# Attention of a conv/SSM, attention and experts kernel in a written order: three batches in flight, sums moved between engines, ranks batch by batch

## The chip, the cores and the metric

The kernel runs on one core of one Trainium2 chip. The metric is device microseconds for one launch. Three runs of the kernel before gave 3556.59 us as their median (3550.72 to 3560.29). Engines are named as in the profile: PE (matrix products and transposes; PEld is its weight load), DVE (vector), ACT (scalar), POOL (GpSimd), SP (which only issues transfers here). Each engine works through its own queue in order and waits on the others by semaphores.

## The reference, cut to what matters

Input is `x` of 4 batches, each 32x32 positions of 256 channels, so 1024 tokens a batch. Layer 0 is a convolution with a state-space scan; it makes up most of the time and is not changed. Layer 1 is attention without a softmax over tokens, then 16 experts of which each token takes two:

```python
# t: (4, 1024, 256); _ln_t: layer norm over the channels
q, k, v = split(_ln_t(t) @ W_qkv + b_qkv)
q = q - mean(q);  k = k - mean(k)                       # over channels
q2, k2 = q*q, k*k
k2 = l2norm(k2 / (sum(k2) + 1e-7), over tokens)
q2 = l2norm(q2 / (sum(q2) + 1e-7), over channels)
kv = einsum('bnc,bnd->bcd', k2, v)
t = t + (v + einsum('bnc,bcd->bnd', q2, kv) / sqrt(N)) @ W_out + b_out
u = _ln_t(t)
probs = softmax(u @ gate_w + gate_b)                    # 16 experts
w, idx = top_k(probs, 2);  w = w / sum(w)
t = t + sum over the two: w * (silu(u @ w1[e]) * (u @ w2[e])) @ w3[e]
```

So per token the kernel needs the sum of squares of q and k, the sum of fourth powers of q, and per channel two sums over all tokens of a batch: of k2 and of k2 squared.

## The kernel before, in words

Tokens lie on the 128 partitions, in groups of 128: a batch is NT = 8 groups, all four together NTA = 32. `t_all` (128 x 32 x 256, fp32) holds the residual stream in SBUF. Everything is fp32.

**The scan** (up to about 2767 us) is ordered by hand. Its last unit leaves four groups (TPB = 4) of the last batch unfinished: `last_half` (L1137) gives them their output product later, inside attention.

**Attention** (L1109 to L1346) is one loop over the batches, L1158. Its order is not written by hand: the framework places the instructions of neighbouring batches on the queues, within what buffers allow. Steps for a batch, with their lines:

- layer norm statistics of the 8 groups on DVE (`statistics`, L1125: `bn_stats` and `bn_aggr`, then a square root on ACT and a reciprocal on DVE); ACT scales the groups to `xh` (L1165); PE transposes them four to a PSUM bank (`transposed`, L114) and DVE copies them out (`xhT`, L1169);
- for each group the q/k product (`pqk`, L1179), the bias on DVE (L1184), both squares in one ACT instruction of 512 elements (`sq`, L1187), both sums by one reduction on DVE (`sums`, L1188), the fourth power with ACT's own accumulator (L1190), the output bias on POOL (L1193), the product of x with W_v W_out (`pv`, L1196) and its addition on DVE (L1200). W_v and W_out are multiplied beforehand, so v is never formed;
- k2 scaled on ACT (L1209) and squared there (`ksq`, L1212); q's norm (L1215 to L1219); q2 transposed, copied out by DVE (`q2T`, L1223);
- the product of k2 with x over tokens (`pkv`, L1231), copied out (L1236); the sums over tokens folded on DVE from 8 groups to 1, for `ksq` and for `k2` (L1241 to L1245), then summed over partitions by PE with a vector of ones (`pkn`, L1251), root and copy (L1254, L1255); the product with W_v W_out, scaled (`kvw`, L1262 to L1269);
- for each group the product of q2 with `kvw` (`po1`, L1276) and its addition, scaled by q's norm (L1280); statistics again; the expert input `xe` on DVE (L1288), stored to DRAM by one transfer of 1 MB (L1292); `xe` transposed, copied out by ACT (L1296); the gate's product (`pgT`, L1303), turned back (`pg`, L1310);
- the gating on DVE with one exponential on ACT (L1311 to L1344): top two of 16 experts as one-hot rows in `hots`, and their weights.

`last_half` is called ahead of the second batch.

**The router** (L1358 to L1463) starts when all batches are gated. It counts the pairs (token, expert) of all 32 groups at once: a 128 x 512 one-hot sum (L1362), two products for totals and for ranks within a group (L1367, L1369), a scan along the groups (L1372), the number of 128-row blocks of each expert and where each expert starts (L1381 to L1386), the expert of each of NBLK = 79 blocks (`eid`, L1389 to L1394), and each pair's slot (L1396 to L1418). Then, in four chunks of 16 groups, it forms one-hot rows of the place in the block (`qh`, L1429) and of the block (`ih`, L1433), and sums group and partition numbers by PE into a list by slot (`pgp`, L1444). `src` and `dst` (L1451 to L1463) are the rows to gather and to scatter.

**The experts** (L1468 to L1568, an order written by hand) go through 74 blocks (more only if needed): SP reads the block's expert from `eid` and loads w1, w2, w3, 512 KB each, four blocks ahead into pools of six buffers (`wp`, opened at L1468, after the router's pools are closed), POOL gathers the block's rows by an indirect transfer (L1488), PE multiplies, POOL scatters the result to `yd` (L1539). **The final sum** (L1572) adds two weighted rows to each token and stores the output.

The order around the change is set by the engines' queues, by the number of buffers of each tile, and by PSUM's banks: `pt` 2, `pq` 3, `po` 2 and `pk` 1.

Of the kernel before, what the change touches and what calls it, by code (L numbers as in the profile page):

```python
# [8 lines left out]
F32 = mybir.dt.float32  # L9
# [24 lines left out]
def conv_ssm_attn_moe_kernel(ctx: ExitStack, tc: tile.TileContext, a: dict, out: bass.AP):  # L34
# [1027 lines left out]
    hots = [l1.tile([P, NTA, NE], F32, name=f"hots{k}") for k in range(2)]  # L1062
# [8 lines left out]
    def counted(n, lo, step, name):  # L1071

        t = l1.tile([P, n], F32, name=name)
        nc.gpsimd.iota(
            t, [[step, n]], base=lo, channel_multiplier=0,
            allow_small_or_imprecise_dtypes=True,
        )
        return t

    nbe = L * NB // BS  # L1080
    bounds = counted(nbe, 0, BS, "bounds")
    blocks = counted(NBLK, 0, 1, "blocks")

    places = l1.tile([P, BS], BF16, name="places")
    nc.vector.tensor_copy(places, counted(BS, 0, 1, "places_f"))
    blocks_h = l1.tile([P, NBLK], BF16, name="blocks_h")
    nc.vector.tensor_copy(blocks_h, blocks)

    groups = l1.tile([P, NTA], BF16, name="groups")
    nc.vector.tensor_copy(groups, counted(NTA, 0, 1, "groups_f"))  # L1090
    part_pk = l1.tile([P, 2], F32, name="part_pk")
    nc.gpsimd.iota(
        part_pk, [[1, 2]], base=1, channel_multiplier=2,
        allow_small_or_imprecise_dtypes=True,
    )
    spare = l1.tile([P, 1], F32, name="spare")
    nc.gpsimd.iota(
        spare, [[1, 1]], base=2 * NB * L + 1, channel_multiplier=1,
        allow_small_or_imprecise_dtypes=True,
    )  # L1100
    before = l1.tile([P, P], F32, name="before_t")
    make_upper_triangular(nc, before, 1.0, diag=False)
    every = l1.tile([P, P], F32, name="every_t")
    nc.vector.memset(every, 1.0)
    keep = l1.tile([P, NE, NTA], F32, name="keep")
    nc.vector.memset(keep, 1.0)
    nc.vector.memset(keep[:, :, 0:1], 0.0)

    with tc.tile_pool(name="wa", bufs=1) as wa, tc.tile_pool(name="att", bufs=1) as att, \  # L1109
            tc.tile_pool(name="sm", bufs=2) as sm, \  # L1110
            tc.tile_pool(name="ps_b", bufs=2, space=PSUM) as ps_b:
        tbs = [t_all[:, b * NT : (b + 1) * NT, :] for b in range(NB)]
        for b in range(NB - 1):
            nc.sync.dma_start(out=tbs[b], in_=rows(td, b))
        nc.sync.dma_start(out=tbs[-1][:, :TPB, :], in_=rows(td, NB - 1)[:, :TPB, :])
        nc.sync.dma_start(out=tbs[-1][:, TPB:, :], in_=rows(xf, NB - 1)[:, TPB:, :])
        wg = load_rows("L1_ffn_gate_w", CK, NE, wa)
        gb = load_bcast("L1_ffn_gate_b", NE, wa)
        iota = wa.tile([P, NE], F32, name="iota")
        nc.gpsimd.iota(  # L1120
            iota, [[1, NE]], base=NE, channel_multiplier=0, allow_small_or_imprecise_dtypes=True
        )
        wqk, wvo, bqk, bvo, bout = made["mats"]

        def statistics(tb, tag, n=NT):  # L1125

            mv = sm.tile([P, n, 2], F32, name="ln_mv", tag=tag + "mv")
            for i in range(n):
                st = sm.tile([P, 6], F32, name="ln_st", tag=tag + "st")
                nc.vector.bn_stats(st, tb[:, i, :])  # L1130
                nc.vector.bn_aggr(mv[:, i, :], st)
            rs = sm.tile([P, n], F32, name="ln_rs", tag=tag + "rs")
            nc.scalar.activation(rs, mv[:, :, 1], AF.Sqrt, bias=eps5)
            nc.vector.reciprocal(rs, rs)
            return mv, rs

        def last_half():  # L1137

            ysb = made["ysb", len(units) - 1]
            _, rs = statistics(ysb, "ln1", TPB)  # L1140
            for j in range(TPB):
                t = tbs[-1][:, TPB + j, :]
                nc.gpsimd.tensor_tensor(t, t, b_o, ALU.add)
                ps = ps_b.tile([P, BANK], F32, name="ps_l", tag="po")
                for m in range(DK):
                    nc.tensor.transpose(ps[:, blk(m, P)], ysb[:, j, blk(m, P)], ident)
                yT = sm.tile([P, BANK], F32, name="yT")
                nc.vector.tensor_copy(yT, ps)
                po = ps_b.tile([P, C], F32, name="po_l", tag="po")
                for m in range(DK):  # L1150
                    nc.tensor.matmul(
                        po, yT[:, blk(m, P)], w_o[:, m, :], start=(m == 0), stop=(m == DK - 1)
                    )
                nc.vector.scalar_tensor_tensor(
                    t, po, rs[:, j : j + 1], t, ALU.mult, ALU.add
                )

        for b in range(NB):  # L1158
            if b == 1:
                last_half()  # L1160
            tb = tbs[b]
            _, rs = statistics(tb, "ln2")
            xh = att.tile([P, NT, C], F32, name="xh", bufs=2)
            for i in range(NT):
                nc.scalar.activation(xh[:, i, :], tb[:, i, :], AF.Copy, scale=rs[:, i : i + 1])  # L1165
            xhT = att.tile([P, CK, L], F32, name="xhT", bufs=2)
            transposed(
                ps_b, xh, NT,
                lambda ck, half, ps: nc.vector.tensor_copy(xhT[:, ck, blk(half)], ps), "pt",  # L1169
            )  # L1170


            sq = att.tile([P, NT, 2, C], F32, name="sq", bufs=2)
            sums = sm.tile([P, NT, 2], F32, name="sums")
            q4 = sm.tile([P, NT], F32, name="q4")
            for i in range(NT):
                pqk = ps_b.tile([P, 2, C], F32, name="pqk", tag="pq", bufs=3)
                for ck in range(CK):
                    nc.tensor.matmul(  # L1179
# [439 lines left out]
```

## Time and profile before

| what | value |
|---|---|
| median of three runs | 3556.59 us (3550.72 to 3560.29) |
| the profiled execution | 3564.42 us, span 3562.6 us, granted PE clock 0.973 |
| scan, to about | 2767 us |
| first q/k product of the four batches | 2779.5, 2841.9, 2912.8 and 2975.0 us |
| first gating step of the last batch | 3034.2 us |
| `src` ready | 3079.4 us |
| first expert product | 3087.7 us |
| last scatter issued | 3520.2 us |
| busy over the whole span | PE 92%, DVE 82%, ACT 78%, POOL 70% |

How to read it: the shares in the last row are means over stages with different limits and hardly speak of attention, which is some 7.5% of the span. The windows are what to read: for a stretch of time, the span, and for each engine its busy time and number of instructions, then PE's granted clock, the share of the transfer engines' time, and GB/s. A group of instructions has its line, engine, operation and shapes, the count, busy time and mean duration, and the idle time of its engine just before. The waits name who waited for whom. Matrix products are pipelined, so their own durations overlap: what one costs in a row of its kind is the time from start to start. DVE's neighbouring instructions overlap by a little in the same way.

### The profile page before, as it was taken

How to read it: one execution, taken by the hardware profiler on the slowest of the kernel's cores; microseconds unless marked ns; L12 is line 12 of the kernel's file. 1: busy time of each engine (PE TensorE's matmuls, PEld its weight loads, DVE VectorE, ACT ScalarE, POOL GpSimd, SP SyncE). 2: the span in 40 equal slices, each digit the busy share in tenths (PEclk: the TensorE clock that was granted, in tenths of full speed). 3: DMA queues.
4: the chain of work that ended last, by engine and by line, in shares of the span. 5: the costliest groups of instructions: out<-in, count | busy, mean ns of one | idle time of the engine just before them, and what ended most of it. 6: DMA issues, size and time to landing. Idle time of an engine off the chain costs nothing.

```text
span 3562.6 us, 62683 instructions
## 1 busy us (share of the span) xinstructions
PE 3292.8 (92%) x23188; PEld 2744.0 (77%) x23188; DVE 2933.6 (82%) x3342; ACT 2764.9 (78%) x4577; POOL 2481.9 (70%) x901
## 2 busy tenths in 40 slices
PE   8999999999999999999999999899999788599995
PEld 4577777887888788878877887788888555498984
DVE  4799999999999999999999999999999776522224
ACT  1799999999999899999999999999999343121110
POOL 0379878987898799879978987998888200133331
PEclk9999999999999999999999999999999899699997
DMA  3332222223332222233332223222222100499996
GB/s 99 108 59 72 61 66 69 70 71 64 76 77 63 73 72 73 67 68 76 71 72 69 67 69 74 61 63 63 67 68 59 59 12 18 157 362 317 301 317 225
DMA packets 423575, 352.38 MB, mean 99 GB/s; under 512 B 194385, under 2 KB 309841, under 8 KB 423266
## 3 DMA queue, kind: packets, MB, share of 16 engines
q1 hardware_dynamic: 403794, 324.56, 31.8%
q0 software_dynamic: 7104, 19.41, 1.6%
q10 hardware_dynamic: 12368, 4.37, 0.5%
q8 instruction: 185, 3.03, 0.3%
q14 instruction: 124, 1.02, 0.1%
HBM read 318.24 MB, written 29.47 MB: 98 GB/s over the span
## 4 chain that ended last, share of the span: by engine, by line
ACT 42%; PE 37%; DVE 9%; DMA 6%; issue 2%; POOL 0%; DVEq 0%; POOLq 0%; ACTq 0%; SPq 0%
ACT da L870 20%; ACT bx L862 18%; PE y L914 8%; PE ps L882 8%; DVE h L893 4%; PE p L1519 4%; DMA yd<-yb,dst 4%; PE ps L877 3%; PE bg L404 2%; DMA xb<-xd,src 2%; PE pf L1531 2%; PE pqk L1179 2%; PE pv L1196 1%; PE ps L404 1%; PE ps_t L120 1%
## 5 line engine op out<-in xcount | busy, mean ns | idle before, releaser
L900 POOL TENSOR_TENSOR h<-h,cb_n 128x2048 f32<-128x2048 f32 x512 | 2143.3, 4193 | 396.6 <-DVE h L893 319.8
L870 ACT ACTIVATE da<-dt,l_conv_a_log_sb 128x512 f32<-128x512 f32 x2048 | 1452.0, 718 | 41.8 <-DVE h L893 40.6
L862 ACT ACTIVATE bx<-dtxT,bT 128x512 f32<-128x512 f32 x1824 | 1308.0, 717 | 17.7 <-DVE dtxT L566 17.7
L893 DVE TENSOR_TENSOR_SCAN h<-da,last,ps 128x512 f32<-128x512 f32 x1024 | 1220.0, 1262 | 27.3 <-PE ps L882 13.6
L914 PE MATMUL y<-ident,h 128*128 128x128 f32 x8192 | 1237.9, 274 | 3.0 <-POOL h L900 3.0
L882 PE MATMUL ps<-ident,bx 128*128 128x128 f32 x7296 | 1171.6, 278 | 74.2 <-DVE h L893 51.7
L893 DVE TENSOR_TENSOR_SCAN h<-da,ps 128x512 f32<-128x512 f32 x1024 | 1170.7, 1201 | 43.1 <-ACT da L870 19.4
L882 PEld LDWEIGHTS ps<-ident,bx 128*128 128x128 f32 x7296 | 854.2, 142 | 299.9 <-DVE h L893 144.9
L914 PEld LDWEIGHTS y<-ident,h 128*128 128x128 f32 x8192 | 968.0, 142 | 3.5 <-POOL h L900 3.5
L877 PE MATMUL ps<-dgb,dtxT 128*128 128x128 f32 x1792 | 387.5, 298 | 31.1 <-DVE h L893 21.9
L877 PEld LDWEIGHTS ps<-dgb,dtxT 128*128 128x128 f32 x1792 | 281.3, 190 | 168.4 <-DVE h L893 88.6
L1525 DVE TENSOR_TENSOR hT<-s,p 128x256 f32<-128x256 f32 x148 | 62.4, 422 | 343.1 <-ACT s L1524 343.1
L1519 PE MATMUL p<-xT,w 128*128 128x128 f32 x2368 | 292.9, 278 | 0.5 <-ACT xT L1508 0.5
L1519 PEld LDWEIGHTS p<-xT,w 128*128 128x128 f32 x2368 | 286.1, 194 | 4.7 <-ACT xT L1508 0.9
L1524 ACT ACTIVATE s<-p 128x256 f32<-128x256 f32 x148 | 56.7, 383 | 277.0 <-PE p L1519 277.0
L1539 POOL DMA_INDIRECT yd<-yb,dst x74 | 73.0, 987 | 271.9 <-DMA yd<-yb,dst 154.5
L404 PE MATMUL bg<-pad,dgc 128*128 128x512 f32 x432 | 221.7, 595 | 2.0 <-ACT yT L642 1.9
L1488 POOL DMA_INDIRECT xb<-xd,src x74 | 72.0, 973 | 133.7 <-DVE dst L1460 109.7
L1531 PE MATMUL pf<-w,hT 128*128 128x256 f32 x592 | 153.5, 382 | 0.1
L1193 POOL TENSOR_TENSOR t_all<-t_all,brow 128x256 f32<-128x256 f32 x32 | 23.2, 747 | 179.7 <-ACT xh L1165 179.7
L1531 PEld LDWEIGHTS pf<-w,hT 128*128 128x128 f32 x592 | 102.2, 193 | 8.2 <-DVE hT L1525 0.5
L1508 ACT COPY xT<-px 128x256 f32<-128x256 f32 x74 | 27.5, 372 | 83.1 <-PE px L1506 83.1
(296 smaller groups left out, 2196.2 us busy)
## 6 DMA issues: line engine op xcount, KB each, us to landing
cb_n<-cd SPq DMA_DIRECT2D x512, 256.0 KB, 3.3
w<-in_L_ffn_w_dram SPq DMA_DIRECT2D x222, 512.0 KB, 6.4
dgc<-diags SPq DMA_DIRECT2D x84, 192.0 KB, 3.1
dgb<-diag_b SPq DMA_DIRECT2D x224, 64.0 KB, 3.1
y<-yd SPq DMA_DIRECT2D x8, 1024.0 KB, 10.2
last<-h SPq DMA_DIRECT2D x256, 2.0 KB, 2.9
diag_b<-zero SPq DMA_DIRECT2D x2, 2048.0 KB, 9.6
xd<-xe SPq DMA_DIRECT2D x4, 1024.0 KB, 4.4
```

What stands on the lines that cost most here:

```text
L404: nc.tensor.matmul(made["bg"].rearrange("p (h w) -> p h w", w=WW), made["dgc", m * 3 + i][:, j, :], pads[m][:, half * ROWS + i : (half + 1 ...
L862: nc.scalar.activation(t, made["dtxT", u][:, j, :], AF.Copy, scale=made["bT", u][:, j, n : n + 1])
L870: nc.scalar.activation(t, made["dt", u][:, m, :], AF.Exp, scale=A[:, m, n : n + 1])
L877: nc.tensor.matmul(t[:, blk(j, P)], made["dtxT", steps[s][0]][:, j, blk(m, P)], made["dgb", s], start=True, stop=True,)
L882: nc.tensor.transpose(t[:, blk(j, P)], made["bx", s, j][:, blk(m, P)], ident)
L893: nc.vector.tensor_tensor_scan(h[:, m, 1:], made.pop(("da", s, m)), made.pop(("dbx", s, m)), 0.0 if seg == 0 else last[b][:, n, m : m + 1] ...
L900: nc.gpsimd.tensor_tensor(h[:, :, :BANK], h[:, :, 1:], over_middle(made["c", s], DK), ALU.mult)
L914: nc.tensor.matmul(made["y", u][j][:, blk(m, P)], made["h", s][:, m, blk(j, P)], ident, is_transpose=True, start=n == 0 and m == 0, stop=n ...
L1488: nc.gpsimd.indirect_dma_start(t, None, xd[:, :], bass.IndirectOffsetOnAxis(src[:, i : i + 1], 0))
L1519: nc.tensor.matmul(p12[:, j, s, :], on[w, i][:, ck, blk(h + j, P)], on["xT", i][:, ck, :], start=(ck == 0), stop=(ck == CK - 1),)
L1531: nc.tensor.matmul(on["pf", i], on["hT", i][:, hk, :], on["w3", i][:, hk, :], start=(hk == 0), stop=(hk == HK - 1),)
L1539: nc.gpsimd.indirect_dma_start(yd[:, :], bass.IndirectOffsetOnAxis(dst[:, i : i + 1], 0), yb, None)
```

## The change

Attention is put under `manual_schedule`, so queues take the instructions in the order of the program, and its steps become small functions that a written loop calls. Iteration `o` finishes batch o (its kv product, `out`), does the q/k part of batch o+1, the gate, routing and ranks of batch o-1, and the statistics and scaling of batch o+2. The last four groups of the scan are turned and multiplied ahead of the first batch's transposes. Batch 0 is loaded in two halves and takes its q/k part by itself, ahead of the loop. The core of the loop, where `n`, `z` and `s` are o+1, o-1 and o+2 if they exist:

```diff
+            turn_next(0); v_out(o, 0); turn_q(o, 0); v_out(o, 1); turn_q(o, 1)
+            first_part(0)                       # q/k of group 0 of batch n
+            turn_e(z, 0); norm_q(o); root(batch[z], "ln3", HT, NT); expert_in(z, 1)
+            turn_next(1); first_part(1); on_with(steps, 2); look_ahead(0, 4)
+            v_out(o, 2); gates(z, 0); turn_e(z, 1)
+            kv(o, 0); on_with(steps, 40); look_ahead(4, 8); gates(z, 1); first_part(2)
+            turn_g(z); steps = route(z)
+            kv(o, 1); on_with(steps, 2); kv_out(o); scale_ahead()
+            v_out(o, 3); on_with(steps, 2); norm_k(o); first_part(3); on_with(steps, 2)
+            kv_w(o); v_out(o, 4); on_with(steps, 1); first_part(4); on_with(steps, 1)
+            k2(n, 0)
+            out(o, 0); on_with(steps, 1); out(o, 1); v_out(o, 5); first_part(5)
+            out(o, 2); on_with(steps, 1); out(o, 3); root(batch[o], "ln3", 0, HT)
+            v_out(o, 6); on_with(steps, 1); first_part(6); expert_in(o, 0)
+            out(o, 4); on_with(steps, 1); first_part(7); v_out(o, 7); fourth(n, 7); k2(n, 1)
+            out(o, 5); on_with(steps, 1); out(o, 6); on_with(steps, 1); out(o, 7)
```

(Joined here to fewer lines; in iteration 0 the missing `z` steps give way to `last_sum` and the constants, and after the last iteration the remaining gate and route steps follow alone.) `on_with(steps, n)` lets the routing of a batch, now a generator of 18 pieces, go on by n pieces.

Work that changes its engine or its form:

```diff
-                nc.scalar.activation(sq[:, i, :, :], qk, AF.Square)
-                nc.vector.tensor_reduce(sums[:, i, :], sq[:, i, :, :], AX.X, ALU.add)
+            for k in range(2):
+                nc.scalar.activation(on["sq"][:, i, k, :], t[:, k, :], AF.Square,
+                    accum_out=on["sums"][:, i, k : k + 1])
...
-                nc.scalar.activation(ksq[:, i, :], k2[:, i, :], AF.Square)
+            nc.gpsimd.tensor_tensor(on["ksq"][:, lo:hi, :], on["k2"][:, lo:hi, :],
+                on["k2"][:, lo:hi, :], ALU.mult)          # four groups at once
...
-                nc.vector.tensor_tensor(four, m[:, : NT // 2, :], m[:, NT // 2 :, :], ALU.add)
-                nc.vector.tensor_tensor(four[:, :2, :], four[:, :2, :], four[:, 2:, :], ALU.add)
-                nc.vector.tensor_tensor(fold[:, k, :], four[:, 0, :], four[:, 1, :], ALU.add)
+                # first half:  two = m[0:2] + m[2:4]                          on GpSimd
+                # second half: two += m[4:6]; two += m[6:8]; fold = two[0] + two[1]
...
-                nc.vector.tensor_scalar(xe[:, i, :], tb[:, i, :], mv[:, i, 0:1], rs[:, i : i + 1],
-                    ALU.subtract, ALU.mult)
+                nc.scalar.activation(on["xe"][:, i, :], tbs[b][:, i, :], AF.Identity,
+                    bias=nm[:, i - lo : i - lo + 1], scale=rs[:, i : i + 1])
```

The expert input is stored by two transfers of 512 KB a batch. The buffers of `sq`, `xe` and `xeT` are their own and single.

Ranks: `route(b)` goes on, after the one-hot rows of its batch, with the sum of both (128 x 128), two products of 128 x 128, a scan over the batch's 8 groups for each expert, the counts of the batches before added (`counts[b]`), each pair's slot within its expert, split into block and place, and the one-hot rows of the places (`qh`, two instructions of 128 x 1024 a batch, kept in SBUF for all batches). What is left for the router after the last batch:

```diff
+        nc.vector.tensor_scalar(nbi, counts[-1], float(BS - 1), None, ALU.add)
+        nc.vector.tensor_single_scalar(nbi, nbi, BS.bit_length() - 1, ALU.arith_shift_right)
...
+        nc.vector.tensor_tensor(
+            pick, hot_all.rearrange("p k g e -> p (k g) e"), over_middle(first, 2 * NTA), ALU.mult
+        )
...
+        nc.vector.tensor_tensor(bh, bf, within, ALU.add)
+        nc.vector.tensor_scalar(done, end, block_p, None, ALU.is_le)
...
+        nc.tensor.transpose(pe, ef, ident)
+        nc.vector.tensor_scalar(eid, pe[:, :NBLK], float(NE - 1), None, ALU.min)
...
-                qh = rt2.tile([P, GC, BS], BF16, name="qh", bufs=2)
-                nc.vector.tensor_tensor(
-                    qh, over_middle(places, GC), over_last(qb[:, k, gs], BS), ALU.is_equal
-                )
```

The four chunks with `ih`, `both` and the products stay. The expert of each block now lies along partitions and is turned by PE into one row. The weights' pool `wp` is opened ahead of the router's pools, so that it shares no memory with them. The constants (number rows, triangular matrix, ones) move from the start of attention into iteration 0.

## The prediction

> **What bounds the kernel now.** I read the windows by stage first (span, then busy PE, PEld, DVE, ACT and POOL, clock, DMA), since the change touches one stretch only: attention with the router (2767.8 to 3080 us), between scan and experts. Whole batches, then the two parts of the router's end:
>
> ```profile
> 2858.00:2915.00 57.00, 48.99 (x191) 31.02 (x191) 35.66 (x84) 23.03 (x56) 5.80 (x8) 0.91 0.06 19
> 2915.00:2977.00 62.00, 53.73 (x209) 34.17 (x208) 42.10 (x107) 25.19 (x61) 5.87 (x8) 0.94 0.05 17
> ...
> 3041.00:3056.00 15.00, 3.37 (x4) 1.18 (x4) 12.43 (x24) 0.00 (x0) 0.00 (x0) 0.61 0.01 2
> 3056.00:3078.00 22.00, 9.14 (x64) 7.90 (x64) 19.67 (x12) 5.41 (x4) 0.00 (x0) 0.50 0.00 0
> ```
>
> A batch takes 62 us; no engine is full, PE (54 with its latencies) is nearest. The router's end is DVE's: 32 busy of 37. The second view cuts one batch into its steps:
>
> ```profile
> 2913.00:2934.00 21.00, 21.00 (x70) 12.49 (x69) 17.94 (x46) 8.35 (x23) 0.00 (x0) 1.00 0.00 1
> 2934.00:2938.00 4.00, 2.42 (x18) 1.70 (x17) 3.84 (x11) 3.29 (x7) 0.00 (x0) 1.00 0.00 0
> 2938.00:2952.50 14.50, 12.10 (x48) 9.29 (x49) 6.63 (x13) 5.37 (x17) 0.00 (x0) 0.88 0.00 0
> 2952.50:2961.60 9.10, 7.72 (x34) 5.47 (x32) 7.80 (x26) 0.00 (x0) 0.00 (x0) 1.00 0.01 2
> 2961.60:2975.00 13.40, 10.49 (x45) 5.09 (x46) 5.83 (x13) 8.18 (x16) 5.87 (x8) 0.87 0.23 78
> ```
>
> Only the first step, q, k and v, fills PE: one token tile each 2.58 us in the timeline, 1.72 for q/k and 0.86 for v. The other 41 us are a chain from engine to engine. The waits (total, times, longest) name its links:
>
> ```profile
> ACT ln_rs L1133 <- DVE ln_mv L1131: 47.2, 5, 12.4
> ACT nk L1254 <- PE pkn L1251: 23.8, 5, 5.9
> DVE xhT L1169 <- PE ps_t L120: 23.4, 4, 7.7
> DVE four L1241 <- ACT ksq L1212: 20.3, 4, 5.1
> ```
>
> So DVE stands until squares of k are done and until the next batch is transposed, and the next batch starts only when this one is gated. Work of another batch could fill these holes.
>
> **The written order: what PE needs.** Per batch, by start-to-start times at full clock: q/k and v 8x2.58 = 20.6; k'x products 32 records x0.215 = 6.9; out products the same 6.9; weighting 1.7; 48 transposes x0.11 = 5.3; gate 8x0.43 = 3.4; its turns, column sums and the new rank products together 2.2. Sum 47. DVE per batch after, by starts (128x512 about 0.62, 128x256 0.35): statistics of input 3.8, evacuations of x and q 5.0, q/k bias 5.0, v 2.8, out with statistics 8x0.86 = 6.9, kv and small ones 3.5, gating 5.5, ranks 5.9 (below): 38. ACT: three squares with accumulators a tile, 24x0.54 = 13 (the fourth-power group shows 0.415 + 0.186, overlapped), two scalings 6.5, expert input 3.4, evacuations 3.2, two table loads 2.6, rest 1.6: 30. POOL from its two rows (128x256 0.75 us, 128x2048 4.19: 1.92 ns an element): squares 2x2.22, six adds of 512 x1.24, folds 2x0.75, bias 8x0.75: 19. So PE becomes the bound, with 47.
>
> What goes from DVE: the sums of squares (32x0.68 = 22 us), the folds (8x2.34 = 19), the expert input (15.6). None shortened PE by itself; they give DVE the room for the new order.
>
> **What it will not reach.** PE waits in its written place for everything made just before: transposes into two banks (0.3 to 0.5 a wait in the timeline), column sums (1.5 now), weights before `out` (0.5 to 1.5), rank products behind DVE. I count 13 such hand-offs of 0.5 in a full iteration, 6.5 us, and 1.5 for GpSimd (below): 8. First and last iteration have less: 5 and 4.6.
>
> GpSimd's new work runs beside DVE. The timeline shows what that can do: eight identical instructions with POOL at work and with POOL idle.
>
> ```profile
> 2962.31 4.31 DVE L1288 TENSOR_SCALAR xe<-t_all,ln_mv,ln_rs 128x256 f32<-128x256 f32 x8
> 2962.52 2.98 POOL L1193 TENSOR_TENSOR t_all<-t_all,brow 128x256 f32<-128x256 f32 x4 [54.73 <-ACT xh L1165]
> ...
> 3023.14 2.68 DVE L1288 TENSOR_SCALAR xe<-t_all,ln_mv,ln_rs 128x256 f32<-128x256 f32 x8
> ```
>
> 1.63 us lost beside 2.98 of POOL, 0.55 each; times 19 us of POOL, at most 10.5 a batch. At the other end, the scan beside a POOL that never rests costs 1.20 to 1.26 (one operand in PSUM), as its groups show: 0. DVE has 9 us of room against PE (47 - 38), so I take 1.5, near the low end: few of the instructions left are of the xe kind, since expert input goes to ACT. The Trainium skill, "SBUF — State Buffer", Who interferes with whom, speaks against the change: an instruction with two SBUF inputs, or in a two-port mode, is blocked for a whole GpSimd instruction, one with an input in PSUM is not. By it only ranks, gating and the one-hot of places collide, some 20 a batch; at half a 1.24 us add each that would be 12 us, DVE at 50 would pass PE's 47, and a full iteration would be near 58.
>
> **The sum for attention** (landing of batch 0, 2767.8, to the last gate's first DVE step, 3034.2: 266.4 now):
> - Head, now 11.7 to the first q/k product. The last half's turns and products come first, in order: chain of copies 0.6, products 1.7, table load 1.28, two scalings 1.7, in all 14.2, and 2.5 for a cold PE (clock 0.50 to 0.71 in these windows): 16.7. In return `last_half` leaves the window 2842 to 2858.
> - q/k of batch 0 alone: PE 13.8, ACT 18.4 (13 + 1.6 + 3.8): 17, ACT's rest passes into the loop.
> - Four iterations: PE 40.9 (no batch behind), 47, 47, 32.4 (none ahead) = 167.3; with waits 5 + 8 + 8 + 4.6: 192.9.
> - From the last `out` to the gate: 11.7 now; half the expert input and transposes are done before, 8.
>
> Sum 234.6: gain 31.8. If no PE wait remained it were 25.6 more.
>
> **Ranks batch by batch.** From the last one-hot (3040.25) to `src` (3079.4) now 39.2 us. What forms the second half, from the DVE groups:
>
> ```profile
> L1429 DVE TENSOR_TENSOR qh<-places,qb 128x2048 bf16<-128x2048 bf16 x4 | 9.1, 2285 | 0.0
> L1437 DVE TENSOR_TENSOR both<-ih,groups 128x1264 bf16<-128x1264 bf16 x4 | 5.9, 1474 | 0.0
> L1433 DVE TENSOR_TENSOR ih<-blocks_h,bh 128x1264 bf16<-128x1264 bf16 x4 | 5.8, 1470 | 0.0
> ```
>
> After, for the last batch alone: sum 0.3, products 0.9, scan on 128 elements 0.36 (not shown; between a 128x128 step at 0.28 and the 512 scan at 1.22, nearer the first), 1.0 for three steps, picks 1.2, slots 0.8, places 2x1.17 = 2.3; then ends 0.9 and 0.2, pick and reduction over 1024 elements 2.4, `bh` and the transposed `eid` 1.0: 11.4 against 15.4. Then four chunks of 2.78 (starts) = 11.1 in place of 20, then 2.3 + 1.9 as now. 26.7: gain 12.5. The first three batches' 5.9 us each lie on DVE under PE. The weights' pool now lies outside the router's, so weight loads follow `eid`, not the end of the router; the first rows' gather took 6.2 us among them. I take 2 us less (between 0 and 3); weights themselves were not late (the first product waited 0.46, for ACT's copy of its rows).
>
> **Small moves.** Batch 0 is loaded by two DMAs, expert input is stored by eight of 512 KB in place of four of 1 MB (4.4 us to landing); SP has nothing else queued until the weights, and the last store lands some 25 us before the first gather: nothing. The constants (nine instructions on POOL, 0.13 to 0.29 each, six on DVE, 1.4 in all) go into iteration 0, where both have room; before, they lay under the end of the scan. POOL's last fold ends an iteration ahead of the first gather in its queue: nothing.
>
> Experts and the final sum keep their instructions; PE is busy 92.5 of 93 in the first expert window, so nothing follows there.
>
> **Sum.** 31.8 + 12.5 + 2 = 46.3. The profiled execution took 3564.42 (span 3562.6), 7.8 above the median of 3556.59; 3518 in its terms, 3510 against the median.
>
> **Rivals.**
> - *PE hardly waits.* For: in the q/k/v step PE shows no hole at all. Waits 4 instead of 25.6, and q/k alone 14: 24.6 more, 3486.
> - *DVE, blocked by GpSimd, sets the pace.* For: the xe rows. DVE 38 + 10.5 and its own in-order waits bring a full iteration back to 62, 7 more, twice, and 6 and 5 in the others: 25 lost, 3535.
> - *Slower: PE's order costs a wait per group.* An order by hand can't step over a late input; the timeline shows today's doing so (gating of one batch among the next one's q/k steps). Some 180 groups of matmuls stand in the four iterations; my waits are 0.14 a group. At 0.40 a group, 72 us, the gain is gone; at 0.5 (the q2T hand-offs of now, everywhere) 90, and 3575. Against: most groups have another batch's input, ready long before.
> - *The change does not do what it says*: the experts absorb the start because loads, not rows, decide. Then 2 to 5 us less; inside the range.
>
> **Chances.** Forecast 0.50, PE without waits 0.22, blocked DVE 0.18, slower 0.07; 0.03 lies near zero. Within 0.3% (10.7 us), about what a measurement of this kernel can tell from no change: 0.03; faster 0.90, slower 0.07. The range reaches from a little under the first rival to a little over the second: 3482 to 3538.
>
> **What would show it.** Right: PE's windows of full iterations near 55 us with 47 of work, clock near 1.0; router end some 27 us with no `qh`; ACT near 60% busy. Wrong: `out` or rank steps on DVE lasting beside POOL; PE waiting on `k2` or `fold`; the first q/k product after 2790. The likeliest error is the size of PE's waits.

## The result, and the profile after

The kernel after takes 3511.88 us (median of four runs, 3511.06 to 3513.99) against 3556.88 (3550.72 to 3560.29): a ratio of 0.9876, 95% interval 0.9859 to 0.9893. The forecast was 3510.

The windows of the kernel after by stage; columns are the stretch, its length, busy PE, PEld, DVE, ACT and POOL with their numbers of instructions, granted clock, DMA share, GB/s. The rows are the head, q/k of batch 0, the four iterations, the last gate, the router, and the first rows' gather.

```profile
2767.80:2785.60 17.80, 13.60 (x66) 10.89 (x66) 5.89 (x21) 9.00 (x19) 3.50 (x5) 0.83 0.52 167
2785.60:2800.20 14.60, 14.60 (x42) 6.90 (x41) 9.33 (x25) 10.34 (x41) 0.37 (x1) 1.00 0.00 1
2800.20:2846.00 45.80, 38.59 (x156) 27.36 (x155) 33.53 (x93) 22.19 (x86) 28.36 (x37) 0.96 0.00 1
2846.00:2903.00 57.00, 51.35 (x225) 34.80 (x224) 40.03 (x119) 30.96 (x98) 18.29 (x18) 1.00 0.07 24
2903.00:2958.00 55.00, 50.11 (x213) 34.24 (x213) 39.31 (x106) 24.38 (x78) 18.30 (x18) 0.97 0.06 20
2958.00:3003.00 45.00, 40.19 (x180) 27.88 (x180) 32.58 (x101) 13.70 (x28) 8.44 (x7) 0.96 0.08 29
3003.00:3011.20 8.20, 5.95 (x20) 2.41 (x20) 3.33 (x9) 5.09 (x10) 0.00 (x0) 0.79 0.19 66
3011.20:3042.30 31.10, 8.58 (x69) 7.28 (x69) 26.68 (x65) 6.40 (x6) 0.05 (x1) 0.62 0.41 142
3042.30:3048.40 6.10, 0.05 (x1) 0.08 (x2) 0.00 (x0) 0.00 (x0) 4.88 (x5) 0.59 1.08 372
```

A full iteration now takes 55 to 57 us where a batch took 57 to 62, and the router 31.1 where it took 46.0 (3034.2 to 3080.2). Of the second half's groups, `qh` is gone from there; `ih` and `both` take 1.47 us as before. PE is nearer to full, and still stands 5 to 7 us in every iteration. The waits of the same kernel name its reasons (in total, times, longest). The first two lines stand beside the chain that was shown of before:

```profile
ACT ln_rs L1149 <- DVE ln_mv L1144: 25.8, 6, 11.6
...
ACT nk L1308 <- PE pkn L1304: 3.7, 2, 2.7
...
PE po L1346 <- DVE t_all L1350: 6.2, 4, 2.7
PE ps_t L1157 <- DVE xhT L1158: 5.8, 3, 3.9
PE ps_t L1157 <- ACT xeT L1158: 2.8, 2, 1.4
PE ps_t L1157 <- ACT xe L1367: 2.7, 7, 1.7
PE pkw L1319 <- DVE ks L1309: 2.6, 3, 1.4
```

ACT's wait for column sums (23.8) is 3.7, and DVE's wait for `ksq` (20.3) is gone with the folds. But PE waits in many small places. The longest single wait, 3.9, comes once, at 2805.2, where the first iteration begins: the turning of q2 needs a bank that DVE's copy of `xhT` has to empty, and DVE stands behind ACT, which is still at the squares of batch 0. The largest in sum is the one for `po`, and the timeline shows how it comes about:

```profile
2898.33 1.89 PE L1346 MATMUL po<-kvw,q2T 128*128 128x256 f32 x8
...
2900.08 0.41 DVE L1340 TENSOR_TENSOR t_all<-pv,t_all 128x256 f32<-128x256 f32 x1
2902.06 0.17 DVE L1242 TENSOR_SCALAR rk<-sums 128x4 f32<-128x4 f32 x1 [1.56 <-ACT sq L1220]
...
2902.36 0.45 DVE L1350 SCALAR_TENSOR_TENSOR t_all<-po,rq,t_all 128x256 f32<-128x256 f32 x1
...
2902.87 1.53 PE L1346 MATMUL po<-kvw,q2T 128*128 128x256 f32 x4 [2.65 <-DVE t_all L1350]
```

`rk` belongs to the next batch and waits for ACT's last square. By the written order it stands ahead of the addition that would free PE's bank, so DVE waits 1.56 us with ready work behind it, and PE 2.65.

**The ledger of the two profiled executions** (spans 3562.6 and 3510.6, 52.0 apart): from 2767.8 to the last gate's first DVE step 266.4 before, 243.4 after, 23.0 gained; router to the first gather 46.0 and 31.1, 14.9; gather to the first turned rows 6.3 and 6.1, 0.2; the rest (experts and final sum) 476.0 and 462.2, 13.8. The medians are only 45.0 apart, since the profiled execution of before was 7.5 us slower than its median.

### The profile page after: what moved, and what is told of

It reads as the page before. It is cut to its first block, busy times and chain, and to the rows that moved or that the text cites. A ratio compares the mean times of both kernels' runs of the same rounds, so it can differ in the third digit from the quotient of the medians.

```text
span 3510.6 us, 62831 instructions
## 1 busy us (share of the span) xinstructions
PE 3267.1 (93%) x23201; PEld 2735.2 (78%) x23201; DVE 2902.2 (83%) x3314; ACT 2779.1 (79%) x4681; POOL 2532.3 (72%) x941
## 3 DMA queue, kind: packets, MB, share of 16 engines
q1 hardware_dynamic: 403874, 324.56, 32.4%
## 5 line engine op out<-in xcount | busy, mean ns | idle before, releaser
L862 ACT ACTIVATE bx<-dtxT,bT 128x512 f32<-128x512 f32 x1824 | 1307.6, 717 | 17.8 <-DVE dtxT L566 17.8
L1248 POOL TENSOR_TENSOR ksq<-k 128x1024 f32<-128x1024 f32 x8 | 15.1, 1892 | 108.6 <-ACT k L1245 93.0
L1766 ACT COPY xT<-px 128x256 f32<-128x256 f32 x74 | 27.6, 372 | 70.2 <-PE px L1764 37.7
```

The source lines that it names most:

```text
L862: nc.scalar.activation(t, made["dtxT", u][:, j, :], AF.Copy, scale=made["bT", u][:, j, n : n + 1])
```

## The experiments

Each ratio is to the kernel before, run on the same chip; the medians of the kernel before on these chips lie between 3556.1 and 3558.4 us. "The loop" is the stretch from the first `pv` product to the last gate's first DVE step: 211.0 us in the kernel after.

**1. The kernel before, profiled again** (nothing edited).

> The kernel before, unchanged, profiled once more. The profiled pair differs by 12.8 us in the expert stage (432.5 against 419.7 us from the first expert product to the end of the last scatter), which the change doesn't touch. Theory 1, that this comes from the execution profiled (it was 7.5 us above the median of its kernel): this profile has a span of 3550 to 3558 us and an expert stage of 422 to 428 us, while the stretch up to the first expert product stays at 3087 to 3088. Theory 2, that the experts really run slower in the kernel before (weights called for in another place): the stage is again 431 us or more, with waits of PE for gathered activations in the middle of the stage.

Measured: 3561.12 us, one run. The stage that was expected at 422 to 428 us took 425.9, as theory 1 said, but the span was 3559.4 and the first expert product came at 3092.1, both later than theory 1 had them. The expert stage as the ledger counts it, from the first turned rows to the end, was 468.4 us against 476.0 in the first profile: 7.6 us of difference in one and the same kernel. So more than half of the 13.8 in the ledger can be variation; 468.4 is still above the 462.2 of after. The attention varies too: the last gate came at 3037.1 against 3034.2.

**2. The order left to the framework.**

```diff
-            tc.tile_pool(name="ps_b", bufs=2, space=PSUM) as ps_b, \
-            tc.manual_schedule():
+            tc.tile_pool(name="ps_b", bufs=2, space=PSUM) as ps_b:
```

> The kernel after with the order of the attention's instructions left to the framework; every instruction, buffer and engine stays as it is. Theory 1, that the gain in the attention is the order's (one batch's products lie beside the next one's chain of statistics and sums): 15 to 35 us are given back, 3527 to 3547 us, with PE's idle time in the attention back near 35 to 60 us. Rival, that the three batches in flight in the program and the moved work are enough and the framework would find as good an order: within 5 us of the kernel after, 3507 to 3517 us.

Measured: 3479.04 us, ratio 0.9785 (0.9767 to 0.9804). Neither expectation: it is 33 us **faster** than the written order. Theory 1 falls: the gain is not the written order's. Windows of this kernel (loop, router, gather), and the four longest of PE's waits from 2778 on (all seven together are 5.6 us):

```profile
2793.00:2976.40 183.40, 177.16 (x789) 121.94 (x787) 127.94 (x385) 93.11 (x279) 59.35 (x55) 1.00 0.07 24
2976.40:3007.50 31.10, 8.58 (x69) 7.28 (x69) 26.27 (x65) 6.41 (x6) 0.03 (x1) 0.62 0.41 142
3007.50:3014.00 6.50, 0.00 (x0) 0.00 (x1) 0.00 (x0) 0.00 (x0) 4.98 (x6) 0.58 1.07 370
```

```profile
PE pg L1393 <- ACT gT L1388: 1.3, 2, 0.7
PE po L1345 <- DVE t_all L1349: 1.2, 1, 1.2
PE ps_t L1156 <- ACT xe L1366: 1.0, 2, 0.8
PE ps_t L1156 <- ACT xeT L1157: 0.7, 1, 0.7
```

And the same loop in the kernel after:

```profile
2800.20:3011.20 211.00, 186.19 (x790) 126.68 (x788) 148.78 (x425) 96.32 (x296) 73.38 (x80) 0.97 0.06 21
```

The same products: PE idle 6.2 of 183.4 against 24.8 of 211.0, and busy 177.2 at a clock of 1.00 against 186.2 at 0.97. The router takes the same and the gather 0.4 more. The loop gives 27.6 us, and the head 5: from the scan's last copy to the first q/k product 12.4 us in place of 17.5.

**3. The moved work alone, in the kernel before.**

```diff
-                nc.scalar.activation(sq[:, i, :, :], qk, AF.Square)
-                nc.vector.tensor_reduce(sums[:, i, :], sq[:, i, :, :], AX.X, ALU.add)
+                for k in range(2):
+                    nc.scalar.activation(
+                        sq[:, i, k, :], qk[:, k, :], AF.Square, accum_out=sums[:, i, k : k + 1]
+                    )
...
+                nc.gpsimd.tensor_tensor(two, m[:, 0:2, :], m[:, 2:4, :], ALU.add)
```

> The kernel before with the moved work alone: the sums of squares of q and k by ScalarE's accumulator in place of VectorE's reduction, the squares of k2 and the sums over the tokens on GpSimd in place of ScalarE and VectorE, the normalised expert input by ScalarE in place of VectorE. The order stays the framework's, two batches, one router behind. Theory 1, that PE waited for a chain and not for VectorE's load: within 10 us of the kernel before, 3547 to 3567 us, as the time taken off VectorE turns into idle time. Rival, that VectorE was the bound of the attention (it loses about 15 us a batch): 20 to 40 us faster, 3517 to 3537 us.

Measured: 3581.76 us, ratio 1.0063 (1.0041 to 1.0084): slower by more than theory 1 had room for, and the rival falls. Where a batch is a chain, a slower engine in the chain makes it longer. The attention from its first q/k products to the last gate, in the kernel before and in this one (DVE's busy time is the third of the five):

```profile
2779.30:3034.20 254.90, 224.38 (x870) 143.83 (x868) 172.62 (x446) 95.44 (x236) 21.99 (x31) 0.93 0.05 17
...
2778.00:3056.00 278.00, 235.49 (x870) 150.98 (x868) 121.62 (x362) 107.02 (x332) 71.20 (x71) 0.87 0.05 16
```

PE's waits in this kernel:

```profile
PE pkn L1256 <- POOL fold L1250: 26.1, 4, 6.5
PE ps_t L120 <- ACT xe L1295: 11.9, 12, 2.7
```

and in the kernel before:

```profile
PE pkn L1251 <- DVE fold L1245: 6.0, 4, 1.5
```

PE waits 20 us more for the token sums, in sum over four batches; the kernel lost 25.6.

**4. Ranks made at once, in the written order.** The router of before (with its `qh` chunks) is put back behind the after kernel's attention, and `route` ends with the weights:

```diff
-            pc = ps_b.tile([P, 2, NE * NT], F32, name="pc", tag="pk", bufs=1)
-            nc.tensor.matmul(pc[:, 0, :], every, flat, start=True, stop=True)
...
+        ptot = ps_r.tile([P, BANK], F32, name="ptot")
+        nc.tensor.matmul(ptot, every, flat, start=True, stop=True)
```

> The kernel after with the ranks of the pairs, their counts and their one-hot rows of places made for all batches at once behind the last batch, as the kernel before does; the attention's order and its moved work stay. Theory 1, that the router's part of the gain is 13 to 15 us and the rank steps inside the iterations hid beside PE's work: 3524 to 3529 us, with the stretch from the last gating step to the first gather at 45 to 46 us against 31.1, and the attention as long as in the kernel after within 2 us. Rival, that VectorE is so full inside the iterations that the rank steps (about 6 us of it a batch) made them longer: the attention gets 6 to 12 us shorter and the whole is 3514 to 3520 us.

Measured: 3522.85 us, ratio 0.9904 (0.9885 to 0.9923). The time is 1 us under theory 1's range; the windows are the rival's, with a loop 10.2 us shorter (loop, router, gather):

```profile
2803.60:3004.40 200.80, 182.26 (x778) 123.78 (x776) 129.50 (x377) 96.29 (x296) 73.36 (x80) 0.98 0.06 22
3004.40:3051.30 46.90, 12.91 (x68) 9.08 (x68) 39.66 (x64) 6.53 (x6) 0.00 (x0) 0.53 0.58 199
3051.30:3054.50 3.20, 0.00 (x1) 0.04 (x1) 0.00 (x0) 0.00 (x0) 2.59 (x3) 0.50 0.26 75
```

The router gives back 15.8, the loop gets 10.2 shorter, and the gather 2.9: 2.7 net. The rest of the 10.2 us between the spans lies elsewhere: this execution ended its scan 4 us later, and its experts took 466.3. In the written order the rank steps are thus not free: they cost the loop about two thirds of what they save.

**5. The same in the framework's order** (experiment 4 without `manual_schedule`).

> The kernel with the framework's order, and the ranks made for all batches at once behind the last. In the written order the rank steps inside the iterations made the attention 12 us longer and the router 16 us shorter. Theory 1, that in the framework's order they cost nothing, since PE is 97 to 99% busy there: the whole 15 to 16 us of the router come back, 3491 to 3497 us. Rival, that VectorE's load by the rank steps costs the attention as much here as in the written order: 3480 to 3485 us.

Measured: 3488.63 us, ratio 0.9809 (0.979 to 0.9829), 9.6 slower than with ranks batch by batch; between the two expectations. Loop, router, gather:

```profile
2794.70:2973.10 178.40, 174.78 (x778) 120.84 (x776) 111.21 (x338) 92.85 (x279) 59.48 (x55) 1.00 0.07 24
2973.10:3019.30 46.20, 12.91 (x68) 9.07 (x68) 39.26 (x64) 6.51 (x6) 0.00 (x0) 0.52 0.57 201
3019.30:3022.40 3.10, 0.00 (x0) 0.00 (x1) 0.00 (x0) 0.00 (x0) 2.45 (x3) 0.50 0.31 96
```

Here the rank steps cost the loop 5.0 us, 2.4 of it PE's own (products of the ranks), and the gather 3.4, and save 15.1 in the router: 6.7 net in these three stretches, 9.6 by the medians. The two intervals overlap by a little, so the gain of ranks by batch is some 7 to 10 us, no more exactly known.

**6. The weights' pool inside, as before.**

```diff
-    wp = ctx.enter_context(tc.tile_pool(name="wp", bufs=6))
...
+    with tc.tile_pool(name="wp", bufs=6) as wp, tc.tile_pool(name="ffn", bufs=2) as ffn, \
```

> The kernel after with the pool of the experts' weights opened with the experts' other pools, as in the kernel before. From the first expert product to the end of the span, the profiles with the pool inside show 476, 468.4 and 474.4 us, those with the pool ahead of the router 462.3, 463.3 and 466.3. Theory 1, that the pool's place makes this difference (the first weights start only when the router's tiles are free): 4 to 12 us given back, 3516 to 3524 us, the stage at 467 to 475. Rival, that it is variation between executions: 3510 to 3514 us.

Measured: 3517.19 us (3514.73 to 3522.65), ratio 0.9894 (0.9873 to 0.9914). The median is 5.3 us above the kernel after, within theory 1, but the intervals overlap. Its stage took 469.2 us. Over all profiles the stage is 468 to 476 with the pool inside (five) and 462 to 470 with it ahead (nine). Some 5 us for the pool's place is likely, not settled. How it would come about is not shown either. The first weight load is issued at 3037.5 here, 0.6 us ahead of the first gather, and 13.4 ahead in the kernel after. Yet in the first 51.6 us of the expert stage PE is as busy here as there, 51.1 us; over the 349 us that follow it falls 5.3 us behind. So it isn't that the first product waits for its weights.

**7. The token sums left out.** Two small operations a batch stand for ten, so the norms of k are not computed.

```diff
-            nc.gpsimd.tensor_tensor(
-                on["ksq"][:, lo:hi, :], on["k2"][:, lo:hi, :], on["k2"][:, lo:hi, :], ALU.mult
-            )
...
-                        nc.gpsimd.tensor_tensor(two, two, m[:, i : i + 2, :], ALU.add)
```

> The kernel after without the squares of k2 and the sums over the tokens (two GpSimd operations on one token tile stand in their place, so the norms of k are not computed). Theory 1, that GpSimd's new work costs by holding VectorE's SBUF-only instructions and by the wait of the weighting for the last sum, about 3 us an iteration: 3498 to 3506 us. Rival 1, that VectorE has room for it and PE doesn't notice: 3509 to 3514 us. Rival 2, that the holding costs 10 us and more an iteration: under 3485 us.

Measured: 3504.88 us, ratio 0.9849 (0.9828 to 0.987). That is in theory 1's range, but the runs spread from 3498.93 to 3510.82, too wide to tell it from rival 1. The loop is the clearer measure (it took 211.0 us in the kernel after and 211.1 in experiment 6, which has the same instructions there):

```profile
2800.10:3005.00 204.90, 184.76 (x790) 124.94 (x788) 139.88 (x424) 96.36 (x296) 25.49 (x45) 0.98 0.06 21
```

6.1 us shorter than 211.0, 1.5 an iteration, half of what theory 1 had, with DVE's same instructions 8.9 us less busy. How much of the 1.5 is the holding and how much the wait for the last sum was not separated. How GpSimd holds DVE is seen in the kernel after:

```profile
2958.44 0.36 DVE L1470 TENSOR_TENSOR pick<-hot_all,run 128x128 f32<-128x128 f32 x1
...
2959.67 1.89 POOL L1248 TENSOR_TENSOR ksq<-k 128x1024 f32<-128x1024 f32 x1 [7.85 <-ACT k L1245]
...
2960.11 1.71 DVE L1470 TENSOR_TENSOR pick<-hot_all,run 128x128 f32<-128x128 f32 x1
```

The same instruction takes 0.36 us alone and 1.71 when it starts under a POOL operation of 1.89. Without the sums the longest of the eight was 0.48. The Trainium skill, "SBUF — State Buffer", Who interferes with whom, says that a vector instruction with both inputs in SBUF is blocked, not slowed, while a GpSimd instruction that reads SBUF has the shared ports. The row agrees: when it starts, 1.45 us of the POOL operation are left, and it ends 0.26 after that.

**8. One step moved in the written order.**

```diff
                 fourth(n, NT - 1)
-                k2(n, 1)
             out(o, 5)
...
             out(o, 7)
+            if n is not None:
+                k2(n, 1)
```

> The kernel after with one step of the written order moved: the second half of the next batch's k2 stands behind the last out step of the iteration and not ahead of out 5. In three of the four iterations VectorE's wait for the last squares then no longer stands ahead of the additions that free PE's banks. Theory 1, that PE's largest waits inside the iterations (2.1 to 2.7 us each for t_all) are the price of that one place: 6 to 9 us less, 3503 to 3506 us. Rival, that VectorE's queue is behind anyway and the wait reappears at the next transposes or at k'x, which now needs k2 later: 3508 to 3516 us.

Measured: 3511.17 us (3505.09 to 3516.28), ratio 0.9867 (0.9844 to 0.9889): the time can't tell it from the kernel after. In the profile the loop is 205.5 us, 5.5 shorter, and the waits are

```profile
PE ps_t L1157 <- DVE xhT L1158: 6.6, 3, 3.9
...
PE po L1346 <- DVE t_all L1350: 2.2, 3, 1.0
```

4.0 us of the wait are gone and 0.8 is back at the transposes. So this place costs a little less than the 6 to 9 us of theory 1 in the one profile; the median does not show it, and this execution's experts took 469.6 against 462.2. It is one place of many.

**9. The framework's order with the token sums on VectorE** (`nc.vector` for `nc.gpsimd` in `k2`, without `manual_schedule`).

> The framework's order, with the squares of k2 and the token sums on VectorE in place of GpSimd. In the framework's order VectorE was busy 124 of the 174 us of the four iterations and PE 171. The sums would take some 7 us of VectorE a batch (two products of 1024 elements at 1.2, six additions of 512 at about 0.6, two of 256 at 0.4), 28 in all: 152 of 174. Theory 1, that PE stays the bound and the place of the sums doesn't matter as long as the order may step over what is late: 3475 to 3485 us. Rival, that VectorE at 87% delays the evacuations that PE waits for: 3488 to 3500 us.

Measured: 3477.14 us, ratio 0.9773 (0.9746 to 0.98), theory 1. The profiled execution (3492.2) was the slowest of the four: its scan ended 8 us later than in experiment 2, and its experts took 4 us more. Its loop took 183.3, as in experiment 2.

**10. The framework's order with nothing moved.**

```diff
-            for k in range(2):
-                nc.scalar.activation(
-                    on["sq"][:, i, k, :], t[:, k, :], AF.Square,
-                    accum_out=on["sums"][:, i, k : k + 1],
-                )
+            nc.scalar.activation(on["sq"][:, i, :, :], t, AF.Square)
+            nc.vector.tensor_reduce(on["sums"][:, i, :], on["sq"][:, i, :, :], AX.X, ALU.add)
...
-                nc.scalar.activation(
-                    on["xe"][:, i, :], tbs[b][:, i, :], AF.Identity,
-                    bias=nm[:, i - lo : i - lo + 1], scale=rs[:, i : i + 1],
-                )
+                nc.vector.tensor_scalar(
+                    on["xe"][:, i, :], tbs[b][:, i, :], mv[:, i, 0:1], rs[:, i : i + 1],
+                    ALU.subtract, ALU.mult,
+                )
```

> The program of three batches in flight in the framework's order, but with all moved work back where it was: sums of squares of q and k by a VectorE reduction, squares of k2 on ScalarE, sums over the tokens and the normalised expert input on VectorE. VectorE's work in the four iterations would be 124 + 28 + 22 (32 reductions at 0.68) + 14 (32 instructions of the expert input at about 0.43) = 188 us against PE's 171 in 174. Theory 1, that the program and not the moved work makes most of the gain, and the moved work is worth what VectorE then lies over PE: 14 to 30 us lost against the framework's order with the moves, 3493 to 3509 us. Rival 1, that the moves are worth nothing: 3476 to 3486 us. Rival 2, that without them nearly all of the gain in the attention goes: over 3525 us.

Measured: 3482.12 us, ratio 0.9791 (0.9763 to 0.9818): rival 1. The loop:

```profile
2789.80:2974.60 184.80, 178.48 (x790) 123.57 (x788) 157.81 (x466) 81.90 (x203) 11.29 (x16) 0.98 0.07 24
```

DVE is busy 158 of 185 us, 30 more than in experiment 2; I had added up 64 more, to 188. PE is as full as with the moves. In this order the moves are worth nothing that can be measured.

**11. The written order with nothing moved** (experiment 10 with `manual_schedule` back).

> The written order of the kernel after, with all moved work back where it was (as in the run before: reductions, token sums and expert input on VectorE, squares of k2 on ScalarE); each piece stands at the written place of the piece that it replaces. Theory 1, that the moves matter only where no instruction may step over another: VectorE gets some 30 us more in four iterations in which it is already the engine that PE waits for, and 15 to 35 us are lost against the kernel after: 3527 to 3547 us. Rival, that the moves are worth as little here as in the framework's order (3 us): 3510 to 3518 us.

Measured: 3577.9 us, ratio 1.0056 (1.0039 to 1.0072), 66 us over the kernel after: about twice theory 1's upper end. The loop:

```profile
2805.40:3073.90 268.50, 197.94 (x788) 134.16 (x788) 188.07 (x510) 83.26 (x213) 13.88 (x20) 0.87 0.05 16
```

Two lines of PE's waits, then lines of the timeline:

```profile
PE po L1342 <- DVE t_all L1346: 45.4, 10, 9.5
PE ps_t L1157 <- DVE xhT L1158: 14.1, 1, 14.1
```

```profile
2878.83 1.49 DVE L1256 TENSOR_TENSOR two<-two,ksq 128x512 f32<-128x512 f32 x2 [2.38 <-ACT ksq L1246]
...
2882.48 0.48 DVE L1346 SCALAR_TENSOR_TENSOR t_all<-po,rq,t_all 128x256 f32<-128x256 f32 x1
...
2883.01 2.07 PE L1342 MATMUL po<-kvw,q2T 128*128 128x256 f32 x4 [8.21 <-DVE t_all L1346]
```

The next batch's token sums stand ahead of this batch's additions. DVE waits for ACT's squares, then does the sums, and PE stands 8.21 us for a bank. The framework, given the same instructions, is 96 us faster (experiment 10). The written places were chosen for the moved work, so what this run shows is the price of this order, not of any order written by hand.

**12. The kernel before with buffers of their own for the expert input** (and one buffer for `sq`, as in the kernel after).

```diff
-            xe = att.tile([P, NT, C], F32, name="xe", tag="xh", bufs=2)
+            xe = att.tile([P, NT, C], F32, name="xe")
...
-            xeT = att.tile([P, CK, L], F32, name="xeT", tag="xhT", bufs=2)
+            xeT = att.tile([P, CK, L], F32, name="xeT")
```

> The kernel before with one thing changed: the normalised expert input and its transpose get SBUF buffers of their own, as in the kernel after, in place of sharing the two of xh and of xhT (and sq has one buffer, as in the kernel after). Its program stays batch behind batch, its order the framework's. Theory 1, that the shared buffers kept the next batch from starting, so that most of the attention's gain is theirs: 15 to 45 us less, 3512 to 3543 us. Rival, that the program's sequence (all of a batch ahead of the next one's first step, which the framework follows) held the next batch back: within 8 us of the kernel before, 3550 to 3566 us.

Measured: 3556.13 us, ratio 1.0004 (0.9993 to 1.0015): the rival. These buffers did not hold the next batch back.

Together, as ratios to the kernel before:

| program | order | work moved | ranks | ratio |
|---|---|---|---|---|
| batch behind batch | framework's | no | at once | 1 |
| batch behind batch | framework's | yes | at once | 1.0063 |
| three in flight | written | yes | by batch (the kernel after) | 0.9876 |
| three in flight | written | no | by batch | 1.0056 |
| three in flight | written | yes | at once | 0.9904 |
| three in flight | framework's | yes | by batch | 0.9785 |
| three in flight | framework's | no | by batch | 0.9791 |
| three in flight | framework's | yes | at once | 0.9809 |

So the program of three batches, its steps given in turn, makes most of the gain; ranks by batch add some 7 to 10 us to it (experiment 5), and the pool perhaps 5. "The program" is here more than the sequence: halves of batches, the place of the scan's last groups and the PSUM banks that a few small tiles use changed with it and were not tried one by one. Written down as a fixed order it loses 33 us of it again, and without the moved work 96. That the framework follows the sequence and steps over what is late is read from these rows and the windows; which of its choices do it was not tried one by one. The fastest is 3477 to 3482 us, experiments 2, 9 and 10, which their intervals don't tell apart.

## Why the prediction was right, point by point

| term | forecast | measured |
|---|---|---|
| head, to the first q/k product | 16.7 | 17.8 |
| q/k of batch 0 | 17 | 14.6 |
| iterations | 45.9, 55, 55, 37 | 45.8, 57, 55, 43.8 |
| last `out` to the gate | 8 | 9.4 |
| attention | 234.6 | 243.4 |
| gain of ranks and router | 12.5 | 14.9 |
| gain at the first gather | 2 | 0.2 |
| experts | 0 | 13.8 in the two profiles |

- **What bounded it** (a chain from engine to engine, not DVE's load) is shown from two sides: with 51 of DVE's 173 busy us in the attention taken off and the sequence unchanged, the kernel loses 25.6 us (experiment 3); with all of that work left on DVE and the sequence changed, PE is busy 178.5 us of a loop of 184.8 (experiment 10).
- **The written order** was not needed for the gain. The prediction looked for the gain in it and did not ask what the framework makes of the same program; experiment 2 shows that: 3479, 33 us less. The gain is the program's. The waits of a written order, which the forecast did price, are what the framework's order mostly avoids (6.2 us of idle PE in the loop against 24.8).
- **PE's need and its waits.** The rows of the four iterations, the last one up to the last `out` addition at 3001.8, show PE idle 7.2, 5.7, 4.9 and 4.5 us, 22.2 in all against 25.6 of waits in the sum. What was mis-sized is PE's busy time: 38.6, 51.4, 50.1 and 39.3, in all 179.4, against 40.9, 47, 47 and 32.4, in all 167.3. In the first three rows too much need and too little waiting, or the reverse, come out within 2 us of the forecast, which is luck; in the last they don't, and it is 6.8 over. The need had been added up at full clock. The loop's products keep PE busy 177.2 us at a clock of 1.00 in experiment 2 and 186.2 at 0.97 here, so some 9 of the 12 us go with the clock; where the rest lies is open.
- **Head and batch 0.** The 14.2 in the head's sum doesn't follow from the four items named beside it, which make 5.3; measured was 17.8 for the 16.7. Batch 0's q/k took 14.6 and not 17, but ACT's rest then shows as PE's wait of 3.9 at the start of the loop.
- **The moved work as "room for the new order"** was right for this written order, and far stronger than I thought: 66 us. In the framework's order it is worth 3, within the intervals. The rival "PE hardly waits", 3486 with 0.22, is what the same program does without its written order: 3479.
- **The slower rival had the right mechanism.** A fixed queue can't step over a late input. Its price is small in the kernel after, 24.8 us of idle PE in the loop. In experiment 11 it went the whole way to 3578; that the rival had 3575 is chance.
- **GpSimd** was taken at 1.5 us an iteration, and experiment 7 gives 1.5, the wait for the last sum included. The row from `xe` would have given up to 10.5. POOL's sums add 8.9 us to DVE's busy time in the whole loop, some 2 a batch. What the Trainium skill, "SBUF — State Buffer", Who interferes with whom, gives for one held instruction agrees with the row above; half an addition for each of 20 a batch, 12 us, was too much.
- **Ranks under PE at no cost** failed. The router gained 14.9, and the rank steps cost the loop 10.2 in the written order (experiment 4), 5.0 in the framework's. This lay hidden in the iterations, three of whose four lengths I had right.
- **The gather's 2 us** failed. Of the first 18 weight loads (9.4 MB), issued from 3028.9 on, four are still to be issued when rows are asked for at 3042.3, and the transfers run at 372 GB/s. With ranks at once the 18 are issued from 3024.6 to 3042.4, the rows are asked for at 3051.3, and the gather takes 3.2 instead of 6.1.
- **Experts at nothing.** Of 13.8 us in the two profiles at least 7.6 can be variation (experiment 1). About 5 may be the pool's place, which I had put on the gather.
- **The sum.** Against the forecast the two profiles give 8.8 less in the attention, 2.4 more in the router, 1.8 less in the gather and 13.8 more in the experts. That the medians come out at 45.0 for 46.3 is luck in part: errors of opposite sign, of which the largest, the experts', is more than half variation between executions.

## What to carry to other kernels

Before an order is written by hand, run the same program with the framework's order: the sequence in which batches' steps are given can be the whole gain, and the fixed order a loss. In a fixed order, look in each engine's queue for an instruction that waits for the next batch's late result ahead of one that frees this batch's bank; PE pays for it twice, as a wait and by the clock. In these runs, work moved off a busy engine gained where that engine's queue held others up (experiment 11 against the kernel after); inside a chain it only put a slower engine in the path (experiment 3).

## What the runs showed of the hardware

- In these runs a pause of PE cost more than its length. The same 788 to 790 products of the loop kept PE busy 177.2 us at a granted clock of 1.00 with 6.2 us idle (experiment 2), 186.2 at 0.97 with 24.8 idle (the kernel after) and 197.9 at 0.87 with 70.6 idle (experiment 11).
- A vector instruction with both inputs in SBUF took 0.36 us alone and 1.71 under a GpSimd multiplication of 1.89. Even so, 48 us less of GpSimd work in the loop took only 8.9 us from DVE's busy time (experiment 7).
- The first gather of rows took 6.1 us beside weight loads at 372 GB/s and 3.1 to 3.2 when these were done (experiments 4 and 5).
- GpSimd's square of 128 x 1024, with one tile as both inputs, took 1.89 us against my 2.22 by size from rows with two tiles; its additions of 512 with two tiles took 1.3 against 1.24.
- The expert input on ACT, with two pointer operands, took 0.59 us a group (four of them 2.06, as neighbours overlap), so 4.1 a batch where 3.4 had been in the sum; ACT, 24 to 31 us busy of 55 to 57, had room for it.
- The scan of 128 x 128 took 0.41 us against an estimate of 0.36; the one-hot of places 1.22 against 1.17.
